# A second Strassen level in the aggregates of the second layer, panels 1 to 4

## The chip, the cores and the metric

One Trainium2 core runs the whole program. The metric is the device time of one execution in microseconds. TensorE (PE, with its weight loads shown apart as PEld) multiplies, VectorE (DVE) adds and evicts, ScalarE (ACT) does the exponentials and some copies, GpSimd (POOL) scales the aggregates and issues the stores, SyncE (SP) issues the loads.

## The reference

A graph network of two attention layers on 2708 nodes with 1024 features. Everything is float32, and the adjacency is a dense 2708 x 2708 integer matrix.

```python
def reference(x, adj, Wf, bf, Wg, bg, W0, bW, W1, a1, a2):
    h = maximum(layernorm(x), 0)
    f, g = h @ Wf + bf, h @ Wg + bg
    e = relu(f @ g.T)
    x = x + softmax(where(adj > 0, e, -9e15), axis=1) @ (h @ W0 + bW)
    h = maximum(layernorm(x), 0)
    hW = h @ W1
    e = leaky_relu(hW @ a1 + (hW @ a2).T, 0.2)
    x = x + relu(softmax(where(adj > 0, e, -9e15), axis=1) @ hW)
    return x
```

The second layer's scores are a sum of a column and a row, so its large products are two: the weights with `h` (the aggregate), and that with `W1` (the projection).

## The kernel before, in words

**Panels.** The destination nodes are cut into five panels, 0 to 4, with 576, 576, 532, 512 and 512 columns. The source nodes are 20 full tiles of 128 rows, which go in ten pairs (`NQ` = 10), and two left-over tiles, `MONO` and `TINY` (20 rows). For each panel of the second layer the kernel makes the exponentials of all source tiles (`weights1`, one item for each tile: two activations on ACT and three wide operations on DVE, into the tiles named P), then `aggregate`, then `project`. The items of the next panel's `weights1` are put into a list, `later`, and taken from it in pieces by `behind(us)`, which is called between the matmuls of the aggregate and of the projection of the panel at hand. `exps_until(n)` takes items until n are done.

**The aggregate** forms G = h^T P, with 1024 features by the panel's columns, in two halves of features (`gT` 0 and 1) of four chunks of 128. It is one level of Strassen's scheme in Winograd's form. In each pair the two source tiles a and b, the two feature halves and the two halves `lo` and `hi` of the columns make 2 x 2 blocks, and seven products M1 to M7 of half the width take the place of eight. The left sides of the seven are made once by `pair_h` and lie in DRAM (`hg_d`, one tensor for each two pairs); they are loaded as `hc`, 512 KB for two pairs, through a pool of 12 stream buffers (`strm`), in program order on SP. The right sides are sums of P, made on DVE in place: `T1` (wa hi minus wa lo), then `second` and `fourth`. Each product is 10 pairs times 4 chunks = 40 matmuls of 128 x 128 by half a panel (288, 266 or 256 columns), and accumulates in four PSUM banks. The order is M1, M5, M2, M6, M3, M7, M4. The results go out by `evict`, and the left-over tiles are added inside M2, M3, M4 and M7.

**The order of work.** PE, SP and DVE each run their queue in order. The order of DVE's queue is made beforehand by a scheduler that estimates when inputs are there; SP's is the program's. There are eight PSUM banks, 54 slots of a panel's width (`slots`), and 12 stream buffers.

**After the aggregate**, `scale` multiplies three quarters of `gT` with the inverse sums on POOL and the last quarter on DVE, and `project` multiplies with `W1`, again by one level of Strassen.

**Names that the change touches.** `pair_h` (left sides of the second layer), `left_h` and `left_over` (left-over tiles), `later`, `put`, `one`, `behind` (the list), `aggregate` (kept for the first layer and for panel 0 of the second), and the loop over panels at the end.

Of the kernel before, what the change touches and what calls it, by code (L numbers as in the profile page):

```python
# [18 lines left out]
P = 128  # L19
# [38 lines left out]
def kernel(  # L58
# [97 lines left out]
    assert sorted(group_of) == list(range(NQ))  # L156
    hg_d = [[dram.tile([P, 7, len(g), W], FP, name=f"hg{l}_d{i}") for i, g in enumerate(groups)] for l in range(2)]
    hsl_d = dram.tile([P, 2, NH, P], FP, name="hsl_d")
    hgl_d = [dram.tile([P, 2, W + P], FP, name=f"hgl{l}_d") for l in range(2)]
    md_d = dram.tile([P, 7, NH, W], FP, name="md_d")  # L160
# [21 lines left out]

    later, credit = [], [0.0]
    ahead = [5]

    def put(us, go, fetch=None, takes_psum=False, ready=None):
        later.append([us, fetch, go, takes_psum, ready])

    def one():
        for it in later[:ahead[0]]:  # L190
            if it[1]:
                it[1]()
                it[1] = None
        us, _, go = later.pop(0)[:3]
        go()
        return us

    def behind(us, psum_free=False):
        credit[0] = min(credit[0] + us, 2 * us)
        while later and credit[0] > 0 and (psum_free or not later[0][3]) and (not later[0][4] or later[0][4]()):  # L200
            credit[0] -= one()

    def flush():
# [97 lines left out]
    def left_h(l, hm, ht):  # L301

        for e in range(2):
            store(hgl_d[l][:, e, :W], hm[e])
            for d in range(NH):
                g = slice(B32 * d, B32 * (d + 1))
                store(hgl_d[l][g, e, W:], ht[e][g, d * P:(d + 1) * P])

    def pair_h(l, q, ha, hb):

        n = P
        on = nc.vector
        if q >= NQ - F // 2:
            s1, s2, s3, s4 = (slot(f"g{i}")[:, :W] for i in range(4))
            i, j = group_of[q]
            for m, h in ((M1, ha[0]), (M2, hb[0]), (M4, hb[1])):
                store(hg_d[l][i][:n, m, j], h)
            on.tensor_tensor(s1, ha[1], hb[1], OP.add)
            on.tensor_tensor(s2, s1, ha[0], OP.subtract)
            for m, h in ((M5, s1), (M6, s2)):  # L320
                store(hg_d[l][i][:n, m, j], h)

            def rest():
                on.tensor_tensor(s4, hb[0], s2, OP.subtract)
                on.tensor_tensor(s3, ha[0], ha[1], OP.subtract)
                for m, h in ((M3, s4), (M7, s3)):
                    store(hg_d[l][i][:n, m, j], h)
            return rest
        g1, g2 = stream("g1", (P, 2, W)), stream("g2", (P, 2, W))
        s1, s2, s3, s4 = g1[:n, 0], g1[:n, 1], g2[:n, 0], g2[:n, 1]  # L330
        on.tensor_tensor(s1, ha[1], hb[1], OP.add)
        on.tensor_tensor(s2, s1, ha[0], OP.subtract)
        on.tensor_tensor(s3, ha[0], ha[1], OP.subtract)
        on.tensor_tensor(s4, hb[0], s2, OP.subtract)
        i, j = group_of[q]
        for m, h in ((M1, ha[0]), (M2, hb[0]), (M4, hb[1])):
            store(hg_d[l][i][:n, m, j], h)
        store(hg_d[l][i][:n, M5:M6 + 1, j], g1[:n])
        store(hg_d[l][i][:n, M7:M3 + 1, j], g2[:n])

    def rows_h(q, ha, hb):

        i, j = group_of[q]
        for m, h in ((M1, ha[0]), (M5, ha[1]), (M2, hb[0]), (M4, hb[1])):
            store(hg_d[0][i][:, m, j], h)

    summed = [0]

    def sums_h():

        def fetch(q, two):
            i, j = group_of[q]
            for m in (M1, M2):
                two.append(stream("hr", (P, 2, W)))
                load(two[-1], hg_d[0][i][:, m:m + 2, j])

        def first(q, two):
            (a0, a1), (b0, b1) = ((t[:, 0], t[:, 1]) for t in two)
            add(b1, a1, b1)
            sub(a1, a0, a1)  # L360

        def second(q, two):
            (a0, a1), (b0, b1) = ((t[:, 0], t[:, 1]) for t in two)
            sub(a0, b1, a0)
            sub(b0, b0, a0)
            i, j = group_of[q]
            store(hg_d[0][i][:, M6:M7 + 1, j], two[0])
            store(hg_d[0][i][:, M3, j], b0)
            store(hg_d[0][i][:, M5, j], b1)
            summed[0] += 1  # L370
        for q in range(NQ):
            two = []
            put(1.4, lambda q=q, two=two: first(q, two), lambda q=q, two=two: fetch(q, two))
            put(1.4, lambda q=q, two=two: second(q, two))

    u = consts.tile([P, NC], FP, name="u")
# [464 lines left out]
    def aggregate(l, p, S, sm, then={}, rate=3.0):  # L841
# [28 lines left out]
        def left(m, q, d):  # L870
            i, j = group_of[q]
            if (m, i) not in hc:
                hc[m, i] = stream("hc", (P, 2, W))
                load(hc[m, i], hg_d[l][i][:, m])
            return hc[m, i][:, j, d * P:(d + 1) * P]

        def left_over(ps, e, s, start=False):


            two = stream("hl", (P, W + P))  # L880
            load(two, hgl_d[l][:, e])
            for d in range(NH):
                nc.tensor.matmul(ps[d], two[:, d * P:(d + 1) * P], S[MONO][:, s], start=start, stop=False,
                                 skip_group_check=True)
            for d in range(NH):
                g = slice(B32 * d, B32 * d + NY)
                nc.tensor.matmul(ps[d], two[g, W:], S[TINY][g, s], start=False, stop=start, skip_group_check=True)

# [42 lines left out]
        def scale():  # L931
            for e, s, k in ((0, slice(0, w), w), (1, hi, h)):
# [5 lines left out]
                                    M4: lambda ps: left_over(ps, 1, lo), (M7, NQ // 2): into_m15})  # L938
        nc.vector.tensor_tensor(of(1, lo), of(1, lo), by(lo, h), OP.mult)
        return [t.rearrange("p (c i) -> p c i", c=NH) for t in G]  # L940

# [338 lines left out]

    done_rows, first_mask, raise_later = {}, {}, []

    def rows_done(t, xt):
# [14 lines left out]
        if panel_of[t] == NP - 1:  # L1298
# [9 lines left out]
            else:  # L1308
# [4 lines left out]
                rest = []  # L1313
                make = lambda: rest.append(pair_h(1, q, *(done_rows[s] for s in pairs[q])))
                if q == NQ - 1:
# [4 lines left out]
                for p in range(1, NP):  # L1320
                    put_max(p, q)
            return

# [12 lines left out]
        elif whole:  # L1336
            put(2.7, lambda: pair_h(1, q, *(done_rows[s] for s in pairs[q])))
            put(0.0, met)

    def halves_of_tiny(name):  # L1340
# [201 lines left out]

    take_weights(0)
    for p in range(NP):
        S, sm = got["P"]
        then = {}
        if p + 1 < NP:
            then = {M3: lambda p=p: take_shifts(p + 1), M7: lambda p=p: take_weights(p + 1)}
        g = aggregate(1, p, S, sm, then, rate=4.0)
        project(1, p, g, finish1(p), by_pair=(p == NP - 1), rate=1.7)  # L1550

# [28 lines left out]
```

## Time and profile before

| | |
|---|---|
| time, median of 3 | 3132.92 us (3130.36 to 3140.1) |
| profiled span | 3135.8 us, 36310 instructions |
| PE busy | 3053.1 us, 97% |
| PE weight loads busy | 2266.1 us, 72% |
| DVE busy | 1835.6 us, 59% |
| ACT, POOL busy | 450.3 us and 427.3 us, 14% each |
| DMA | 666.04 MB, 212 GB/s on average |

An fp32 matmul stands in the profile as two records, each with a weight load of its own. [...] neighbours overlap; the rate of a run of records is read from the start of one group to the start of the next. The second layer runs from about 2157 us to the end: five aggregates of 132 to 152 us and five projections of 48 to 62 us. Busy time of an engine in a stretch counts overlapping instructions once.

### The profile page before, as it was taken

To read this page: it belongs to the slowest core of one execution; us is meant where nothing else is said; L and a number is where in the kernel's file an instruction comes from. 1 tells how busy PE (TensorE), PEld (TensorE's weight loads), DVE (VectorE), ACT (ScalarE), POOL (GpSimd) and SP (SyncE) were. 2 spreads that over 40 slices of the span, in tenths; PEclk is the share of its full clock that TensorE was granted. 3 is DMA by queue.
4 is the path that set the end of the run, shared out by engine and by line. 5 is a ranking of instruction groups with operands and counts; after the bars stand their busy time and mean duration, and the time that the engine had idled before them with its cause. 6 is when DMAs were issued, how large, how long until landed. Compare 5 with 4: busy or idle time off the path is not lost.

```text
span 3135.8 us, 36310 instructions
## 1 busy us (share of the span) xinstructions
PE 3053.1 (97%) x12694; PEld 2266.1 (72%) x12694; DVE 1835.6 (59%) x3767; ACT 450.3 (14%) x785; POOL 427.3 (14%) x654
## 2 busy tenths in 40 slices
PE   8998999899999999999999999998999999999998
PEld 4576777657877588886888885875757758678684
DVE  5766693776741686426973377758573571745612
ACT  3420020010200101101020002103131130311200
POOL 1421101310002110023000101021010020120202
PEclk9999999999999999999999999998999999999999
DMA  6989967988546796468955678597655565565655
GB/s 220 294 252 248 292 247 253 301 275 230 175 136 156 222 247 223 149 153 253 284 180 160 171 214 245 191 293 250 200 179 175 158 200 158 171 197 172 219 169 181
DMA packets 386278, 666.04 MB, mean 212 GB/s; under 512 B 171744, under 2 KB 212224, under 8 KB 386096
## 3 DMA queue, kind: packets, MB, share of 16 engines
q1 hardware_dynamic: 341936, 536.96, 56.9%
q0 software_dynamic: 44160, 126.76, 12.6%
q8 instruction: 101, 1.65, 0.2%
q14 instruction: 81, 0.66, 0.1%
HBM read 548.26 MB, written 115.30 MB: 212 GB/s over the span
## 4 chain that ended last, share of the span: by engine, by line
PE 81%; issue 6%; DVE 6%; DMA 5%; SPq 1%; POOL 1%; ACT 0%; POOLq 0%; DVEq 0%; ACTq 0%
PE gz L617 11%; PE gx L617 11%; PE gy L617 10%; PE sz L1140 6%; PE pz L1029 5%; PE gv L617 5%; PE sx L1140 4%; PE sy L1140 4%; PE px L1029 4%; PE py L1029 4%; PE M_ps L530 3%; PE qz L617 2%; PE qx L617 2%; PE qy L617 2%; DVE junk L45 1%
## 5 line engine op out<-in xcount | busy, mean ns | idle before, releaser
L1140 PE MATMUL sz<-B,As 128*128 128x288 f32 (+2 forms) x1200 | 295.9, 396 | 12.1 <-DVE st L45 7.9
L1140 PEld LDWEIGHTS sz<-B,As 128*128 128x128 f32 x1200 | 229.4, 192 | 63.1 <-DVE st L45 11.8
L933 POOL TENSOR_TENSOR gT<-gT,rr 128x2304 f32<-128x2304 f32 (+5 forms) x20 | 73.0, 3648 | 1081.4 <-DVE rr L45 979.3
L1140 PE MATMUL sx<-B,As 128*128 128x288 f32 (+2 forms) x800 | 201.5, 395 | 11.2 <-DMA As<-hs_d 9.1
L1140 PE MATMUL sy<-B,As 128*128 128x288 f32 (+2 forms) x800 | 199.3, 392 | 0.0
L617 PE MATMUL gz<-Sa,hc 128*128 128x288 f32 (+2 forms) x800 | 190.3, 399 | 5.9 <-DMA hc<-hg_d 5.9
L617 PE MATMUL gx<-P,hc 128*128 128x288 f32 (+2 forms) x800 | 187.0, 394 | 0.1
L617 PE MATMUL gz<-P,hc 128*128 128x288 f32 (+2 forms) x800 | 185.5, 392 | 0.0
L1140 PEld LDWEIGHTS sx<-B,As 128*128 128x128 f32 x800 | 152.5, 191 | 45.2 <-DMA As<-hs_d 10.1
L617 PE MATMUL gy<-T,hc 128*128 128x288 f32 (+2 forms) x800 | 184.2, 391 | 0.0
L617 PEld LDWEIGHTS gz<-Sa,hc 128*128 128x128 f32 x800 | 154.6, 194 | 40.0 <-DMA hc<-hg_d 6.4
L617 PEld LDWEIGHTS gx<-P,hc 128*128 128x128 f32 x800 | 152.4, 191 | 34.2 <-issue 3.7
L1140 PEld LDWEIGHTS sy<-B,As 128*128 128x128 f32 x800 | 152.3, 191 | 30.8
L617 PEld LDWEIGHTS gz<-P,hc 128*128 128x128 f32 x800 | 151.3, 190 | 31.6 <-issue 1.8
L617 PEld LDWEIGHTS gy<-T,hc 128*128 128x128 f32 x800 | 152.0, 190 | 30.5
L1029 PE MATMUL pz<-w,ps 128*128 128x512 f32 x320 | 142.1, 594 | 0.8 <-DVE pt L45 0.8
L1029 PE MATMUL py<-w,ps 128*128 128x512 f32 x320 | 141.9, 593 | 0.0
L1029 PE MATMUL px<-w,gT 128*128 128x512 f32 x320 | 141.0, 593 | 0.0
L143 POOL DMA_DIRECT2D out_dram<-x_res x180 | 89.2, 502 | 269.7 <-DVE x_res L45 264.5
L1029 PEld LDWEIGHTS pz<-w,ps 128*128 128x128 f32 x320 | 60.2, 190 | 77.1 <-issue 71.0
L1029 PEld LDWEIGHTS py<-w,ps 128*128 128x128 f32 x320 | 60.6, 190 | 75.5 <-issue 73.1
L530 PE MATMUL M_ps<-wgT,wfT 128*128 128x512 f32 x256 | 112.9, 597 | 1.6 <-ACT hsT L45 1.6
(319 smaller groups left out, 4894.9 us busy)
## 6 DMA issues: line engine op xcount, KB each, us to landing
hc<-hg_d SPq DMA_DIRECT2D x350, 512.0 KB, 3.7
As<-hs_d SPq DMA_DIRECT2D x150, 512.0 KB, 5.2
w<-wt_d SPq DMA_DIRECT2D x96, 512.0 KB, 4.9
w<-in_L_gnn_W_dram SPq DMA_DIRECT2D x72, 512.0 KB, 4.8
md<-md_d SPq DMA_DIRECT2D x56, 512.0 KB, 5.7
adj_i<-in_adj_dram SPq DMA_DIRECT2D x200, 128.0 KB, 5.2
hs_d<-hsT POOLq DMA_DIRECT2D x40, 512.0 KB, 7.2
As<-hs_d SPq DMA_DIRECT2D x50, 256.0 KB, 4.8
```

The source lines that it names most:

```text
L45: i = f(*a, **k)
L143: nc.gpsimd.dma_start(a, b)
L530: nc.tensor.matmul(ps, wfT[a][c // NH][:, c % NH, :], wgT[b][c], start=(c == 0), stop=(c == NC - 1))
L617: nc.tensor.matmul(ps[d], left(m, k, d), right(m, k), start=(start and k == 0), stop=(k == K - 1), skip_group_check=True)
L933: nc.gpsimd.tensor_tensor(of(e, s), of(e, s), by(s, k), OP.mult)
L1029: nc.tensor.matmul(ps, left[i][m][:, k, :], w_[k], start=(start and k == 0), stop=(k == NH - 1), skip_group_check=True)
L1140: nc.tensor.matmul(ps[:n, :h], lefts[q][:, i % 2, c, :n], B[m][c // 2][:, c % 2, :h], start=(start and c == 0), stop=(c == NH - 1), skip_g ...
```

## The change

For panels 1 to 4 of the second layer each of the seven products is split once more by the same scheme. Two neighbouring pairs (2k and 2k+1, so five k) are the inner dimension, each feature half is cut into two quarters of 256, and each half panel into two of 144, 133 or 128 columns. A product of 40 matmuls becomes seven of 5 x 2 = 10 matmuls of half the columns, which is 49 small products for each panel.

- `pair_h` writes its left sides as blocks into one tensor, `hr_d`, in pieces of 1 KB. `put_quarters` makes the four further left sums of each m and k: it loads 512 KB through POOL's queue, does four subtractions or additions of 128 x 256 on DVE, and stores 512 KB into `hs2_d`. These 35 items go into a second list, `lazy`, which is served when `later` is empty.
- `quarters_of` makes the right sides. `make(m)` does 5 x 4 subtractions of 128 x 144 (133, 128) for each of the seven m. The first set and the `T1` are made during the projection of the panel before.
- `aggregate_quartered` runs the 49 products. Each loads 512 KB (`hc2`) for four of the five k; the fifth comes from two further loads of 512 KB for each m (`hl2`, in pieces of 1 KB). A bank holds both chunks of one quarter. The results of M1 and M5 are built in their place in `gT`; those of the others in two tiles V, and then added to it.
- The calls of `behind` are one for each small product, with 1.2 us; the next panel's shifts and weights are taken at M7 and M3 in place of M3 and M7 (the order of the two has changed too).
- Panel 0 keeps the old aggregate, and reads the new layout.

```diff
+    hr_d = dram.tile([P, 7, 2, 2, NK, WH], FP, name="hr_d")
+    hs2_d = dram.tile([P, 7, 4, NK, WH], FP, name="hs2_d")
...
+        while not later and lazy and credit[0] > 0:
+            credit[0] -= one(lazy)
...
+    def put_quarters(m, k):
+        two = []
+        def fetch():
+            two.append(stream("hq", (P, 4, WH)))
+            nc.gpsimd.dma_start(two[0], hr_d[:, m, :, :, k].rearrange("p h f c -> p (h f) c"))
+        def go():
+            a11, a12, a21, a22 = (two[0][:, i] for i in range(4))
+            add(a22, a21, a22)
+            sub(a21, a11, a21)
+            sub(a11, a22, a11)
+            sub(a12, a12, a11)
+            store(hs2_d[:, m, :, k], two[0])
...
+        put(1.7, go, fetch, to=lazy)
...
+        def make(m):
+            for k in range(NK):
...
+                sub(t[M5], r12, r11)
+                sub(t[M6], r22, t[M5])
+                sub(t[M7], r22, r12)
+                sub(t[M4], r21, t[M6])
...
+        def product(m, n, ps, start):
+            quarters_until(m)
+            if (m, 0) not in lasts:
...
+                    lasts[m, i] = stream("hl2", (P, 4, WH))
+                    load(lasts[m, i], of)
+            t = stream("hc2", (P, NK - 1, WH))
...
+            for k in range(NK):
+                for d in range(2):
+                    lhs = t[:, k] if k < NK - 1 else last
+                    nc.tensor.matmul(ps[:, d], lhs[:, d * P:(d + 1) * P], inner_right(m, n, k),
+                                     start=(start and k == 0 and d == 0), stop=(k == NK - 1), skip_group_check=True)
+            behind(fine)
...
+        for m in BY_QUARTERS:
...
+            X = bank2("gx")
+            product(m, M1, X, True)
+            nc.scalar.copy(c21, X)
+            if left_out:
+                left_out()
+            Z = bank2("gz")
+            product(m, M6, Z, True)
+            add(c12, Z, c21)
+            Y = bank2("gy")
+            product(m, M5, Y, True)
+            add(c22, Y, c21)
...
+            if m in before_next:
+                before_next[m]()
+            product(m, M2, X, False)
...
+            product(m, M7, Z, False)
+            add(c22, Z, c22)
+            product(m, M3, Y, False)
...
+            add(c12, Y, c12)
...
+            into_place(m, V, 0)
+            def left_out(m=m, V=V, Z=Z, c21=c21):
+                product(m, M4, Z, False)
+                add(c21, Z, c21)
+                into_place(m, V, 1)
...
+            if m == M5:
+                of_right["second"]()
...
-        g = aggregate(1, p, S, sm, then, rate=4.0)
-        project(1, p, g, finish1(p), by_pair=(p == NP - 1), rate=1.7)
+        g = aggregate_quartered(p, S, sm, next_right, then) if p else aggregate(1, p, S, sm, then, rate=4.0)
+        hooks = {}
+        if p + 1 < NP:
+            next_right = quarters_of(p + 1, got["P"][0])
+            hooks = {M7: next_right["first"], M4: next_right["fifth"]}
+        project(1, p, g, finish1(p), hooks, by_pair=(p == NP - 1), rate=1.7)
```

## The prediction

> **What bounds the kernel now.** I read the page first (busy time and chain), then the busy time by stage, then the timelines of PE and DVE in single stages.
>
> ```profile
> PE 3053.1 (97%) x12694; PEld 2266.1 (72%) x12694; DVE 1835.6 (59%) x3767; ACT 450.3 (14%) x785; POOL 427.3 (14%) x654
> PE 81%; issue 6%; DVE 6%; DMA 5%; SPq 1%; POOL 1%; ACT 0%; POOLq 0%; DVEq 0%; ACTq 0%
> ```
>
> The chain that ended last is PE for 81%. By stage of the second layer, from panel 1 on (aggregate, projection, aggregate and so on; columns: length, then busy time of PE, PEld, DVE, ACT, POOL, then clock, DMA share, GB/s):
>
> ```profile
> 2357.10:2507.30 150.20, 150.20 (x645) 115.72 (x644) 63.64 (x123) 20.98 (x38) 11.60 (x10) 1.00 0.53 162
> 2507.30:2569.00 61.70, 61.70 (x145) 27.32 (x144) 40.81 (x63) 20.23 (x33) 14.12 (x29) 1.00 0.55 170
> 2569.00:2707.40 138.40, 138.40 (x641) 115.36 (x640) 59.02 (x118) 19.01 (x34) 11.47 (x12) 1.00 0.56 175
> 2707.40:2760.30 52.90, 52.90 (x241) 24.20 (x240) 38.60 (x63) 18.50 (x33) 19.99 (x40) 1.00 0.65 205
> 2760.30:2893.60 133.30, 133.30 (x641) 115.37 (x640) 57.34 (x117) 18.86 (x34) 10.81 (x10) 1.00 0.59 181
> 2893.60:2941.70 48.10, 48.10 (x114) 21.29 (x114) 38.19 (x60) 17.32 (x29) 11.85 (x24) 1.00 0.69 209
> 2941.70:3073.70 132.00, 132.00 (x630) 114.16 (x629) 34.59 (x79) 6.73 (x14) 10.79 (x10) 1.00 0.59 183
> ```
>
> PE has no gap in any of these stages, so what PE does not have to do is gained, unless something new makes it wait. DVE is busy 43% of an aggregate, but 80% of the short projections.
>
> The rate of PE, from panel 3, and short transposes from panel 2:
>
> ```profile
> 2777.58 17.43 PE L617 MATMUL gy<-T,hc 128*128 128x256 f32 x80
> 2794.84 13.98 PE L617 MATMUL gx<-P,hc 128*128 128x256 f32 x64
> ...
> 2685.95 0.60 PE L238 MATMUL sp_ps<-ident,z 128*128 128x128 f32 x4
> 2686.39 0.60 PE L238 MATMUL sp_ps<-ident,none 128*128 128x128 f32 x4
> ```
>
> From start to start 80 records of 256 columns take 17.26 us, 215.8 ns each. The same view gives 242.5 ns at 288 columns (19.40 us for 80) and 224.1 ns at 266 (17.93 us). The slope is (242.5 - 215.8)/32 = 0.834 ns a column, the rest 2.3 ns. The four transposes are 128 columns with a new weight tile each, and take 0.44/4 = 110 ns.
>
> DVE back to back, in panel 2 and in projection 0:
>
> ```profile
> 2573.22 3.20 DVE L45 TENSOR_TENSOR T<-P 128x266 f32<-128x266 f32 x9
> 2314.06 0.69 DVE L45 TENSOR_TENSOR ps<-ps,gT 128x512 f32<-128x512 f32 x1
> 2314.67 0.69 DVE L45 TENSOR_TENSOR ps<-gT 128x512 f32<-128x512 f32 x1
> 2315.27 0.68 DVE L45 TENSOR_TENSOR ps<-gT,ps 128x512 f32<-128x512 f32 x1
> ```
>
> One of 266 columns takes (3.20 - 0.43)/8 = 0.346 us from start to start, one of 512 takes 0.60. So an independent fp32 operation costs about 0.067 us and 1.05 ns a column: 0.20 us at 128 columns, 0.21 at 133, 0.22 at 144, 0.34 at 256, 0.37 at 288. One that needs its neighbour's result starts about 0.1 us later.
>
> [...] the weight loads of an fp32 pair stand 0.11 us apart where two follow each other ("26.73 0.30 ... x2" with 0.19 for one), though each lasts 190 ns. [...] The trace has 401 and 416 GB/s in stretches of 5 us at a share of 1.02.
>
> **PE, the gain.** An aggregate has 7 x 80 = 560 records now and 49 x 20 = 980 after, of half the columns. By the line above they take 122.4 ns at 144, 113.2 at 133, 109.1 at 128; [...] the transposes show 110 for such a pair. So panel 1 goes from 135.8 to 120.0 us, panel 2 from 125.5 to 110.9, panels 3 and 4 from 120.8 to 106.9: 15.8 + 14.6 + 13.9 + 13.9 = 58.2 us less. The left-over MONO matmuls have the same columns (twice as many at half width). The TINY ones, 0.71 us for eight now, become four short groups; I put 0.2 us more for each of four places, 3 us in all. Net 55.
>
> **DVE, what it adds.** A panel gets 140 subtractions of a quarter, 140 x 0.21 to 0.25 = 29 to 35 us. Evictions go from 28 of half a panel to 42 of the same size, and 16 twice as wide into place, which is 14 x 0.35 + 16 x 0.62 = 15 us. Aggregate 3 then has 57 + 32 + 15 - 3 (T1, moved) = 101 us of DVE work in about 107, and projection 3 has 38 + 4 + 3 = 45 in 48. It fits on average with little to spare, so the order decides.
>
> **The start of each quartered aggregate, the wait I expect.** The queue order of the changed program shows what lies ahead of the first eviction. In panels 2 to 4 DVE, after the last eviction of the projection (0.3 us into the aggregate), has: seven operations of exponential items, ten T1 subtractions, one x_res, three subtractions of `second` (10 us by the rows above), then 15 of the 20 quarter sums of M5 and two wide operations (5 us), and only then c12, the eviction of the M6 product. So c12 is done at about 15.4 us. PE needs it for the M7 product, which accumulates in the same bank, after M1, M6, M5 and M2: 4 x 2.18 = 8.7 us. PE waits 6.7 us. Behind it the M3 product waits 0.4 us for c22, the M4 product 0.2, the next M7 and M3 0.9 together, as DVE works off `second` (20 x 0.34) and the second set of sums; after 45 us DVE has caught up. That is 8.2 us for each of panels 2 to 4. In panel 1 only 13 operations more than the quarter sums stand ahead, c12 comes at 12 us and perhaps 2 later, against 4 x 2.45 = 9.8; with the follow-ups 5 us. Sum 30 us. What is queued behind c12 on DVE is exponentials and sums; ACT's copies of the next X wait with them, and mask loads on SP that need a freed slot, with `hc2` loads behind them.
>
> **Loads.** An aggregate's left sides go from 35 to 63 loads of 512 KB, +14.7 MB. Panel 3 moves 181 GB/s x 133 us = 24.1 MB now, 38.8 MB after, in about 115 us: 337 GB/s, against 401 to 416 measured at full share. Eight or so products of lookahead lie in the 12 buffers. I expect short waits, 1 us a panel: 4 us.
>
> **First layer and panel 0.** 35 items add 140 x 0.34 = 48 us of DVE and 36.7 MB of DMA, spread over 1500 us in which DVE is 60% busy; PE hides them, but where a list was empty an item's load and its first use are issued together, and DVE waits for a load of some 5 to 7 us in its queue. I take 3 us (0 to 10). The 1 KB pieces of `hr_d`, the wider `hgl`, the copies on ACT (19 of 133 us busy) and the POOL scaling (7 us, now issued some 14 us before the projection) lie beside PE work: nothing.
>
> **Sum.** 3132.9 - 55 + 30 + 4 + 3 = 3115 us.
>
> **Rivals.** (a) DVE is quicker than I count or its order harmless, and PE keeps nearly all: 3132.9 - 55 + 4 + 3 = 3085, down to 3078. For it: DVE's busy sum is under PE's time everywhere. Against: the order of the queue. Chance 0.22. (b) Small waits in many places, each product being only 2.2 us long where it was 17 to 20: with twice my DVE waits on panels 1 and 3 and 5 us more for loads, +18, so 3133, no change. Chance 0.14. (c) Transfers or weight loads become the bound. At 300 GB/s, the best of the 78 us slices, 38.8 MB take 129 us, and an aggregate of panel 3 or 4 ends 14 us later than I have it, panels 1 and 2 somewhat less: +45, so 3160. And if the weight loads (190 ns long) [...] set 125 ns a record, panels 2 to 4 would gain 3, -2 and -2 us and panel 1 would gain 13, 45 us lost: 3160. For both: a DMA share of 0.59 that would go to about 0.9, and no run of full-width fp32 pairs under 215 ns in this trace. Against: 401 GB/s and 110 ns are seen. Chance 0.22. The forecast itself has 0.42.
>
> **How the numbers follow.** The forecast is the sum with its DVE waits, 3115. The range reaches down to the full gain (3078, rounded to 3082) and up to the load-bound case with a part of it avoided, 3155. Faster by over 0.3% means under 3123.5: forecast and (a), 0.63 with the forecast's upper tail taken off and some of (b) added. Within 0.3%: 0.14. Slower: 0.23.
>
> **What would show each step.** PE records of 128 columns at 109 to 112 ns from start to start within a product (0.19 us would break the gain). In panels 2 to 4, a gap of PE of 5 to 8 us ahead of the second gz group of each aggregate, put down to DVE gT. An aggregate 3 of 107 + 9 us. A DMA share near 0.85 with few PE waits for hc. No new idle time in the projections and little before 2157 us. The forecast is wrong if PE waits for loads over 10 us a panel, or if DVE's gap is absent.

## The result, and the profile after

The changed kernel takes 3185.9 us (median of 4, 3176.1 to 3189.4) against 3131.6: a ratio of 1.0166, 95% interval 1.0142 to 1.0190. It is slower by 1.7%, where 3115 us and a gain were forecast.

Part 1 of the page of the changed kernel (busy time, share of the span, instructions), and the summary of its chain:

```profile
PE 3030.0 (95%) x14630; PEld 2319.2 (73%) x14630; DVE 2072.4 (65%) x4587; ACT 462.3 (15%) x817; POOL 488.9 (15%) x724
PE 69%; DVE 13%; DMA 9%; issue 6%; SPq 2%; ACT 1%; POOL 1%; POOLq 0%; DVEq 0%; ACTq 0%
```

PE is busy 23 us less and the profiled execution takes 52 us more, so PE waits: its share of the chain fell from 81 to 69%, and DVE and DMA took it. The busy time by stage of the second layer, the changed kernel (length, busy PE, PEld, DVE, ACT, POOL, clock, DMA share, GB/s). The first line is panel 0's aggregate, which is not split; the others answer to the lines shown of before:

```profile
2201.40:2368.02 166.62, 160.00 (x663) 121.61 (x664) 125.28 (x250) 41.74 (x71) 20.38 (x19) 0.95 0.70 225
2416.08:2565.30 149.22, 139.06 (x1128) 136.82 (x1127) 105.06 (x278) 19.54 (x39) 11.95 (x10) 0.95 0.79 251
2565.30:2627.10 61.80, 61.80 (x146) 27.36 (x145) 42.12 (x76) 17.99 (x29) 14.06 (x29) 1.00 0.63 197
2627.10:2762.51 135.41, 127.41 (x1126) 125.48 (x1125) 103.24 (x274) 24.18 (x45) 12.17 (x12) 0.97 0.84 276
2762.51:2815.41 52.90, 52.90 (x243) 24.20 (x242) 39.40 (x76) 16.46 (x29) 19.88 (x40) 1.00 0.73 231
2815.41:2948.61 133.20, 125.18 (x1125) 123.47 (x1124) 100.75 (x274) 23.77 (x45) 11.49 (x11) 0.97 0.87 286
2948.61:2996.68 48.07, 48.07 (x114) 21.29 (x113) 38.25 (x69) 16.04 (x26) 11.79 (x24) 1.00 0.74 234
2996.68:3127.18 130.50, 123.00 (x1114) 121.45 (x1112) 84.06 (x247) 15.76 (x32) 11.07 (x10) 0.97 0.88 288
```

Two things are to be seen. The second layer starts at 2201.40, where before it started at 2147.94: the loss of 53.5 us is complete before the first split product runs, and panel 0's aggregate adds 5.5 (161.1 before). And the four split aggregates gain almost nothing: 150.2, 138.4, 133.3, 132.0 became 149.2, 135.4, 133.2, 130.5, together 5.6 us. Their PE time fell by 8 to 11 us each, but PE no longer fills the stage, and the clock is 0.95 to 0.97. The four projections shown or named here are as long as before (48.1, 61.8, 52.9 and 48.1 us); what follows the last aggregate went from 62.1 to 60.4 us.

**What PE waits for in the first layer.** From the view of PE's waits up to 2201 us (us in total, times, longest), first after, then before. `sx`, `px` and the like are PSUM banks of the scores and the projection:

```profile
PE sx L1368 <- DMA As<-hs_d: 34.7, 8, 9.2
PE px L1257 <- DMA w<-in_L_gnn_W_dram: 16.5, 1, 16.5
```
```profile
PE sx L1140 <- DMA As<-hs_d: 9.1, 2, 8.1
```

The left sides `As` of the scores and the weights `w` come late. Up to the start of the second layer PE is idle 40 us longer than before, and its 8760 records, as many as before, keep it busy 13 us longer (2095.8 us against 2082.7); together that is the 53.5. The instants are those at which the new items (`put_quarters`) run: their 35 loads stand in the trace at 698 to 719, 1159 to 1188, 1564 to 1595, 2093 to 2113 and 2233 to 2288 us, seven at a time, and 23 us of the `As` waits end at 715, 735, 1170 to 1206 and 1592, the `w` wait at 2148; the other 11.7 come before the first item, as the 9.1 of before do. Busy time in the first two of these stretches (columns as above), after, then before, and in the first of them in the run `spread` told below:

```profile
690.00:740.00 50.00, 39.70 (x140) 28.99 (x139) 41.07 (x93) 0.00 (x0) 14.38 (x20) 0.87 0.98 297
1150.00:1205.00 55.00, 45.91 (x202) 37.66 (x200) 47.49 (x106) 0.00 (x0) 13.59 (x18) 0.96 1.01 299
```
```profile
690.00:740.00 50.00, 48.41 (x192) 37.37 (x193) 39.40 (x87) 0.00 (x0) 4.16 (x7) 0.97 0.96 258
1150.00:1205.00 55.00, 55.00 (x247) 46.63 (x246) 37.65 (x83) 0.00 (x0) 2.86 (x4) 1.00 0.97 284
```
```profile
690.00:740.00 50.00, 49.27 (x204) 38.31 (x203) 36.28 (x74) 0.00 (x0) 2.71 (x6) 1.00 0.93 250
```

The DMA engines were full here before the change: a share of 0.96 and 0.97, though at 258 and 284 GB/s only. A burst of seven items adds 7.3 MB to that, PE loses 9 us of busy time in each stretch, and the granted clock falls, to 0.87 in the first.

**What PE waits for in a split aggregate.** The seven small products of a product bear the names M1 to M7 too, and run in the order M1, M6, M5, M2, M7, M3, with M4 put behind the first one of the next group; "the M5 group" below is the seven of the large M5, the second group of an aggregate. c21, c12 and c22 are quarters of a group's result. PE's timeline at the start of panel 1's aggregate, then ScalarE's and VectorE's over the same time (rows left out):

```profile
2420.99 2.12 PE L1059 MATMUL gy<-quarter,hc 128*128 128x144 f32 x16
2431.92 4.21 PE L1059 MATMUL gx<-P,hc 128*128 128x144 f32 x16 [8.32 <-ACT gT L45]
2436.83 2.12 PE L1059 MATMUL gz<-quarter,hc 128*128 128x144 f32 x16
```
```profile
2424.81 0.76 ACT L45 ACTIVATE P<-vb,f2s 128x576 f32<-128x576 f32 x1
2430.90 0.68 ACT L45 ACTIVATE P<-P 128x576 f32<-128x576 f32 x1 [5.33 <-DVE P L45]
2431.49 0.38 ACT L45 COPY gT<-gx 128x288 f32<-128x288 f32 x1
```
```profile
2425.55 3.03 DVE L45 TENSOR_TENSOR T<-P 128x288 f32<-128x288 f32 x8
2429.16 0.81 DVE L45 SCALAR_TENSOR_TENSOR P<-ub,f,P 128x576 f32<-128x576 f32 x1
2430.11 0.75 DVE L45 TENSOR_TENSOR P<-P,maskl 128x576 f32<-128x576 f32 x1
```

The fourth small product (M2) adds into the bank of the first, so it needs that bank copied out to c21. The product ended at 2418.7. ScalarE copies it only at 2431.5: in its queue an exponential stands ahead, which waits for the masking that VectorE ends at 2430.9, and VectorE works through the sums of M1, T1 and other exponentials without a pause. PE waits 8.3 us here, and 6.1, 6.1 and 7.1 us in panels 2 to 4. And when it starts, 16 records take 4.21 us and not 2.12: half speed, for 4.9 us, at a granted clock of 0.50 (2432 to 2436 us).

### The profile page after: what moved, and what is told of

The parts are those of the page before. It is cut to its first block, busy times and chain, and to the rows that moved or that the text cites. A ratio compares the mean times of both kernels' runs of the same rounds, so it can differ in the third digit from the quotient of the medians.

```text
span 3187.6 us, 41503 instructions
## 1 busy us (share of the span) xinstructions
PE 3030.0 (95%) x14630; PEld 2319.2 (73%) x14630; DVE 2072.4 (65%) x4587; ACT 462.3 (15%) x817; POOL 488.9 (15%) x724
## 4 chain that ended last, share of the span: by engine, by line
PE 69%; DVE 13%; DMA 9%; issue 6%; SPq 2%; ACT 1%; POOL 1%; POOLq 0%; DVEq 0%; ACTq 0%
PE sz L1368 5%; PE gy L654 5%; PE gz L1059 5%; PE gx L654 5%; PE gz L654 5%; PE pz L1257 4%; PE px L1257 4%; PE sx L1368 4%; PE gx L1059 4%; PE gy L1059 3%; PE py L1257 3%; PE sy L1368 3%; PE M_ps L567 3%; PE gv L654 2%; PE qz L654 2%
## 5 line engine op out<-in xcount | busy, mean ns | idle before, releaser
L1368 PE MATMUL sx<-B,As 128*128 128x288 f32 (+2 forms) x800 | 209.7, 407 | 36.5 <-DMA As<-hs_d 34.7
L1059 PE MATMUL gz<-quarter,hc 128*128 128x128 f32 (+2 forms) x1344 | 168.8, 279 | 0.4 <-DVE gT L45 0.4
L1059 PEld LDWEIGHTS gz<-quarter,hc 128*128 128x128 f32 x1344 | 160.9, 191 | 1.2 <-DVE gT L45 0.6
L1257 PE MATMUL py<-w,ps 128*128 128x512 f32 x320 | 142.0, 593 | 0.0
L970 POOL TENSOR_TENSOR gT<-gT,rr 128x2304 f32<-128x2304 f32 (+5 forms) x12 | 44.4, 3699 | 560.1 <-DVE rr L45 522.0
L1257 PEld LDWEIGHTS px<-w,gT 128*128 128x128 f32 x320 | 61.2, 194 | 89.6 <-issue 87.8
L1059 PE MATMUL gx<-P,hc 128*128 128x128 f32 (+2 forms) x640 | 88.2, 295 | 27.6 <-ACT gT L45 27.6
L654 PE MATMUL gy<-T,hc 128*128 128x288 f32 (+2 forms) x480 | 111.6, 394 | 0.0
L1059 PEld LDWEIGHTS gx<-P,hc 128*128 128x128 f32 x640 | 83.6, 204 | 31.6 <-ACT gT L45 28.4
```

The lines of the kernel that those rows point to most:

```text
L654: nc.tensor.matmul(ps[d], left(m, k, d), right(m, k), start=(start and k == 0), stop=(k == K - 1), skip_group_check=True)
L970: nc.gpsimd.tensor_tensor(of(e, s), of(e, s), by(s, k), OP.mult)
L1059: nc.tensor.matmul(ps[:, d], lhs[:, d * P:(d + 1) * P], inner_right(m, n, k), start=(start and k == 0 and d == 0), stop=(k == NK - 1), ski ...
L1257: nc.tensor.matmul(ps, left[i][m][:, k, :], w_[k], start=(start and k == 0), stop=(k == NH - 1), skip_group_check=True)
L1368: nc.tensor.matmul(ps[:n, :h], lefts[q][:, i % 2, c, :n], B[m][c // 2][:, c % 2, :h], start=(start and c == 0), stop=(c == NH - 1), skip_g ...
```

## The experiments

Each kernel below was timed beside the kernel before, whose median was 3128.3 to 3133.2 us in these sessions, so medians of different sessions are best compared by their ratios. Stage lengths come from PE's timeline of one profiled execution of each, as the distance between the first records of stages; "first" is the start of the second layer, a0 to a4 are its aggregates. Panels 2 to 4 repeat to 0.4 us between kernels that do the same there, panel 1 to 2.3. The first layer's end moves by some 8 us between such kernels, and the whole time of one kernel by 12 (3121.7 to 3134.3 in the 12 executions of `spread`). The first four projections kept 48.1, 61.8, 52.9 and 48.1 us in all of them.

| run | median us | ratio, 95% interval | first | a0 | a1 | a2 | a3 | a4 |
|---|---|---|---|---|---|---|---|---|
| before | 3131.6 | 1 | 2147.9 | 161.1 | 150.2 | 138.4 | 133.3 | 132.0 |
| changed | 3185.9 | 1.0142-1.0190 | 2201.4 | 166.6 | 149.2 | 135.4 | 133.2 | 130.5 |
| no_items | 3118.8 | 0.9964-0.9985 | 2135.3 | 161.8 | 147.4 | 135.4 | 133.2 | 130.5 |
| copies | 3159.2 | 1.0089-1.0119 | 2176.1 | 162.0 | 147.6 | 135.4 | 133.1 | 130.5 |
| own_bufs | 3219.1 | 1.0282-1.0313 | 2233.0 | 162.0 | 149.7 | 135.4 | 133.2 | 130.5 |
| spread | 3126.6 | 0.9981-1.0005 | 2146.2 | 161.3 | 149.7 | 135.4 | 133.2 | 130.5 |
| own12 | 3223.4 | 1.0264-1.0297 | 2239.4 | 162.0 | 148.9 | 135.8 | 133.5 | 130.4 |
| no_items_10 | 3136.9 | 1.0005-1.0023 | 2162.7 | 160.9 | 148.7 | 135.6 | 133.4 | 130.5 |
| burst_late | 3163.8 | 1.0094-1.0127 | 2130.2 | 199.5 | 149.7 | 135.4 | 133.2 | 130.5 |
| spread_start | 3147.3 | 1.0034-1.0051 | 2147.4 | 161.6 | 143.8 | 145.1 | 141.9 | 134.1 |
| spread_warm | 3157.8 | 1.0054-1.0084 | 2148.5 | 161.9 | 151.0 | 143.0 | 140.6 | 138.6 |
| no_sums | 3113.7 | 0.9938-0.9967 | 2144.4 | 161.6 | 146.5 | 133.2 | 131.5 | 126.8 |
| pool_t1 | 3155.8 | 1.0069-1.0103 | 2147.3 | 161.1 | 154.4 | 141.7 | 140.4 | 137.8 |
| pool_both | 3168.8 | 1.0114-1.0145 | 2147.0 | 160.9 | 157.6 | 145.5 | 147.3 | 140.7 |
| early | 3143.7 | 1.0031-1.0061 | 2147.3 | 161.3 | 154.6 | 139.2 | 137.2 | 130.5 |
| whole1 | 3116.9 | 0.9945-0.9974 | 2152.5 | 161.8 | 140.8 | 134.1 | 132.8 | 129.1 |
| whole2 | 3107.1 | 0.9918-0.9948 | 2145.1 | 161.7 | 141.9 | 130.5 | 127.8 | 124.1 |
| best2 | 3101.3 | 0.9896-0.9929 | 2141.1 | 161.2 | 142.0 | 130.5 | 127.8 | 124.1 |

### The first layer: items, bytes, buffers or layout

**no_items**

```diff
-        put(1.7, go, fetch, to=lazy)
+        return
...
-            load(t, hr_d[:, m, i // 2, i % 2, :NK - 1] if raw else hs2_d[:, m, i, :NK - 1])
+            load(t, hr_d[:, m, i // 2, i % 2, :NK - 1])
```

> Left out: the quarter sums of the left sides (the 35 items that load a group of hr_d, subtract and store hs2_d); the products that would read hs2_d read hr_d in its place, so loads, matmuls and evictions of the second layer are as many as in the changed kernel. The layout of hr_d in pieces of 1 KB stays. Theory A (the tiles of the items hold places of the 12 load buffers, and the one load queue waits in order for them) and theory B (their 36.7 MB come when the DMA engines are full): the first layer ends at 2148 us as before and not at 2201, whole time about 3133, and 5 us less if the first aggregate of the second layer is relieved too. Theory C (the layout, 1 KB pieces instead of 2 KB, slows the stores): the first layer still ends near 2195, whole time about 3180.

3118.8 us, 67 less than the changed kernel (60 by the ratios). The items cost the whole of the loss; the layout of `hr_d` costs nothing (theory C falls). That this first layer ends 12.6 us earlier than before was not expected and stays unexplained; part of it may be the scatter.

**copies**

```diff
         def fetch():
-            two.append(stream("hq", (P, 4, WH)))
-            nc.gpsimd.dma_start(two[0], hr_d[:, m, :, :, k].rearrange("p h f c -> p (h f) c"))
+            nc.gpsimd.dma_start(hs2_d[:, m, :, k], hr_d[:, m, :, :, k].rearrange("p h f c -> p (h f) c"))
         def go():
-            a11, a12, a21, a22 = (two[0][:, i] for i in range(4))
...
-            store(hs2_d[:, m, :, k], two[0])
+            nc.gpsimd.dma_start(hs2_d[:, m, :, k], hr_d[:, m, :, :, k].rearrange("p h f c -> p (h f) c"))
```

> Changed in content: each item copies its group from hr_d to hs2_d twice, inside DRAM, with no tile, no DVE work and no sums; the bytes queued are as in the changed kernel (512 KB twice an item). Theory A (buffers): with no tile in the ring the first layer ends near 2150, whole time about 3135. Theory B (transfers): the engines have the same to move at the same moments, so the first layer ends near 2195, whole time about 3180.

3159.2, between the two: transfers alone, with no tile and no sum, cost 40 us over no_items. That price is near that of the items' own transfers and not the same: a copy reads and writes DRAM both times (35 times 512 KB, 18 MB, more each way), and the second doesn't wait for sums. The rest, 19 us by the ratios and 27 by the medians, belongs to the tiles, the sums and the waits between them.

**own_bufs**, **own12** and **no_items_10**

The edit is that of own_bufs. own12 keeps 12 buffers in `strm` and takes the room from `slots` (51 in place of 54); no_items_10 is no_items with 10 buffers in `strm`.

```diff
-    strm = ctx.enter_context(tc.tile_pool(name="strm", bufs=12))
+    strm = ctx.enter_context(tc.tile_pool(name="strm", bufs=10))
+    hqs = ctx.enter_context(tc.tile_pool(name="hqs", bufs=2))
...
-            two.append(stream("hq", (P, 4, WH)))
+            two.append(hqs.tile([P, 4, WH], FP, tag="hq", name="hq"))
```

> The tiles of the items get 2 buffers of their own, and the ring of loads has 10 in place of 12. Theory A: the load queue no longer waits for the stores of hq; most of the 53 us come back, whole time 3140 to 3150 (the smaller ring may cost some). Theory B: the same transfers at the same moments, 3180 to 3190.

> The tiles of the items get 2 buffers of their own, and the ring of loads keeps its 12; the room comes from the slots, 51 in place of 54. The run of copies showed that the bytes alone cost 40 us over the run without items, and the changed kernel 67; this asks after the other 27. Theory A2 (places of the ring held by hq until the stores have landed): 3155 to 3165. Theory H (VectorE's 48 us of sums, in program order in the scores, and waiting for their loads): 3180 to 3190.

> The run without items (quarter sums of the left sides left out, hr_d read in the place of hs2_d) with a ring of 10 load buffers in place of 12. If places of the ring are what is scarce in the first layer, this alone costs some 35 us and more (3118 to 3150 or above), and explains why 2 buffers of their own for the items made the time longer, 3219. If a place more or less costs nothing, 3118 to 3124, and that run needs another cause.

Both kernels with buffers of their own are slower than the changed one, by 33 and 38 us (41 and 36 by the ratios): theory A failed as it was put. A ring of 10 explains some 12 us by the ratios (0.9974 to 1.0014; 18 by the medians), but own12 has the ring of 12. Its waits from 600 to 2260 us show what happened instead:

```profile
DVE hq L45 <- DMA hq<-hr_d: 87.6, 19, 10.3
```
```profile
PE sx L1369 <- DVE sm L45: 46.6, 8, 15.8
```

In the changed kernel these are 9.4 and 1.8 us. The load queue's waits for the items' stores fell from 42.3 to 1.9 us, and none of PE's waits in the scores is for `As` any more. But a burst of seven now goes through two places: in the first one, loads 3 to 7 are issued at 722 to 749 us, each 4 to 8 us after a store was issued (714 to 742 us). VectorE, whose order is the written one in the scores, stands before these loads with the right sides `sm` and the evictions of the scores behind it, and PE waits for those. So these runs exchange one wait for another, and how the last 19 to 27 us divide between ring and VectorE stays open; in own12 the three slots fewer may cost some as well.

**spread**

```diff
-        while not later and lazy and credit[0] > 0:
-            credit[0] -= one(lazy)
...
             if by_k:
                 behind(rate)
+                in_gaps(2 if rate == 4.0 else 1)
```

> All computed as in the changed kernel; the items no longer run in a burst of seven when the list is empty, but one after each of the seven products of a first-layer aggregate, and two after each product of the second layer's first aggregate, where DVE and DMA have room (DMA share 0.55 to 0.65 there before, 0.9 to 1.0 at the start of the scores). Theories A and B alike: the waits for As and w go, the first layer ends at 2150 to 2158, the first aggregate of the second layer takes 161 to 168 us, whole time 3135 to 3145. Theory C: about 3180. A burst that moves its waits to hc loads of the aggregates would show as waits of gx, gy, gz for hc.

3126.6, with all that the changed kernel computes: some 8 us better than both theories had it. The first layer ends at 2146.2, panel 0's aggregate is 161.3 as before. The waits of the load queue and of VectorE for the items are longer than ever:

```profile
SPq L139 <- DMA hs_d<-hq: 159.2, 31, 12.3
```
```profile
DVE hq L45 <- DMA hq<-hr_d: 86.7, 16, 9.7
```

The load queue waits 159 us for stores of the items, where it waited 68 in the changed kernel, and VectorE stands 87 us before their loads, as long as in own12. The kernel is within 8 us of the one without items all the same: no wait of PE for `As` is left after 600 us, and one of 4.7 us for `w`. What an item holds is not the price; what stands behind it at that moment is.

**burst_late**

```diff
-                in_gaps(2 if rate == 4.0 else 1)
+                in_gaps(0 if m != M5 else 14 if rate == 4.0 else 7)
```

> In the run with spread items, the items come in bursts of seven again, but behind the second product (M5) of each first-layer aggregate, where the DMA share was 0.5 to 0.65 before, and 14 in one go at the same place of the second layer's first aggregate. Theory N (it is the place: at the start of the scores the DMA engines were already full, and PE has little loaded ahead): the first layer ends at 2145 to 2155 as with spread items, whole time 3125 to 3140. Rival O (it is the burst itself: seven items take places of the ring and delay what is behind, wherever they stand): the first layer ends at 2175 or later, with waits of gx, gy, gz for hc, whole time 3155 or more.

Theory N in the first layer: bursts of seven, at 852, 1250 and 1628 us, where the DMA share was 0.44 to 0.48 before, and the first layer ends at 2130 (in an execution 11 us under the median, so perhaps 2141). The 14 at once in panel 0's aggregate cost 38 us (199.5), with waits for `hc` there that `spread` doesn't have:

```profile
PE gx L657 <- DMA hc<-hr_d: 24.8, 3, 17.4
```

So a burst of seven cost nothing that shows where the engines had that room. The 14 differ in size and in place, and which of the two makes their price wasn't tried.

### The second layer: the wait at the start of an aggregate

All of these stand on `spread`.

**spread_start**

```diff
-            behind(fine)
...
-        before_next = {M1: lambda: make(M5), M5: with_second,
+        before_next = {M1: lambda: of_right["fifth"](), M5: with_second,
...
+            nc.hold = ("vector", "scalar") if m == M1 else ()
             product(m, M1, X, True)
             nc.scalar.copy(c21, X)
+            behind(fine)
...
```

> The run with spread items, and in each quartered aggregate another order of the first seven products: items of exponentials are called after the evictions, not before; the ten subtractions of `fifth` come after c22 of the M5 product and the sums of M5 after the second c22; VectorE and ScalarE keep that written order through the first group. Theory D (the copy of the first small product to c21 stands on ScalarE behind an exponential that waits for VectorE, and PE waits 8.3, 6.1, 6.1 and 7.1 us for it, then runs some 5 us at half clock): all four gaps fall under 1 us, each aggregate of panels 1 to 4 is 8 to 11 us shorter, 149.7 to 139, 135.4 to 127, 133.2 to 125, 130.5 to 122, whole time 3126 - 36 = 3090. Rival E (VectorE as a whole has too much to do; the wait comes back at the next eviction): the gaps move to gz or gy and the aggregates keep 147, 133, 131, 129; whole time 3118 to 3126.

Rival E. Panel 1 gained 5.9 us, its gap fell from 8.3 to 1.0. In panel 2 the first gap went too, and 8.2 us came at c21 of the next group, M5, whose copy stood again behind an exponential that waited for VectorE; the last M3 product of panels 1 to 3 waited some 5 us in place of 1 to 2. Panels 2 to 4 lost 9.7, 8.7 and 3.6.

**spread_warm**

```diff
+            if m == M1:
+                dull = bank("dull")
+                for _ in range(26):
+                    nc.tensor.matmul(dull[:, :P], ident, ident, start=True, stop=True, skip_group_check=True)
             product(m, M2, X, False)
```

> The run with spread items, and 26 matmuls of the identity by itself (52 records, 5.7 us by 110 ns) that nothing reads, put into a bank of their own ahead of the product that waits for c21 in each quartered aggregate. They fill the gap and remove none of it. Theory F (the half clock after a gap is a cost of its own, some 2.4 us a gap): the product after starts as late as before but at full clock, each aggregate of panels 1 to 4 is 2 to 2.5 us shorter (149.7 to 147.4, 135.4 to 133, 133.2 to 130.9, 130.5 to 128.2), 9 us in all, though PE has more to do. Rival G (the slow records belong to the busy memory, not to the clock): the products after the gap stay at twice their time and the aggregates are as long as before or longer.

The half speed is the clock's (0.50 granted over the 3.8 us after this gap in the changed kernel): in panel 2 the wait for c21 shrank to 0.31 us and the 16 records behind it took 2.08 us where 6.1 us of waiting had made them 3.9 (rival G falls). In panel 1, where 2.50 us of waiting were left, the 16 records still took 3.72 us. But nothing was won. PE came to the next eviction earlier and waited 1.76 us there, and 5.82 us in the M5 group; the aggregate was 7.6 us longer. VectorE's order moved with the added matmuls as well, so this run doesn't price the clock.

**no_sums**

```diff
-                four = slot("quarter", (P, 4, WX // 4))
...
+                t = {}
...
```

> Left out: the 140 subtractions of a panel that make the quarter sums of the right sides (the products read the quarters themselves); all else as in the run with spread items, with the same matmuls, loads and evictions. Theory K (VectorE works without a pause over the first 30 us of a quartered aggregate, 40 of the sums among it, so PE waits for it wherever one looks; moving the wait or the clock does not help, removing VectorE work does): the four gaps of 6 to 8 us and the half clock after them go, the aggregates take 149.7 to 137-139, 135.4 to 124-127, 133.2 to 121-124, 130.5 to 119-121, whole time 3126 - 45 = 3080. Rival L (the gap is the order on ScalarE alone, exponentials and T1 still stand ahead of c21): gaps of 4 us remain and the aggregates lose 5 to 6 us each, 3103.

Nearer to rival L: gaps of 5.1, 4.0, 3.9 and 3.8 us in place of 8.3, 6.1, 6.1 and 7.1, about as it has them, and 1.7 to 3.7 us an aggregate, less than it has. So the sums made some 11 us of the 27.6; the other 17 stay when they are gone, and exponentials and T1 are what is left ahead of c21.

**pool_t1** and **pool_both**

```diff
-                sub(t1(q), wa_(q)[:, hi], wa_(q)[:, lo])
+                nc.gpsimd.tensor_tensor(t1(q), wa_(q)[:, hi], wa_(q)[:, lo], OP.subtract)
```

> The ten T1 subtractions of a panel (`fifth`) on GpSimd in place of VectorE, in the run with spread items; VectorE has 3.8 us less ahead of the first evictions. Theory K: each gap shrinks by 3 to 4 us, the aggregates by 4 to 5 us, whole time about 3110. If GpSimd's own queue (stores of the output rows that wait for VectorE stand ahead) brings T1 late, the wait moves to the sums of M5 and nothing is won: 3125 to 3135.

> As the run before, and the 20 quarter sums of M1 on GpSimd too: 8.8 us off VectorE around the start of each quartered aggregate. GpSimd scales 1024 columns in 2.34 us, so 20 sums of 128 to 144 columns should take some 8 to 10 us there. Theory K: gaps near 0 and aggregates of 140, 127, 125, 122, whole time about 3095. Against it: the M6 product, the second of an aggregate, needs these sums 2.2 us after the start, and if GpSimd has them late PE waits for it instead: 3125 to 3150.

pool_both moves the sums of M1 as well. Both lose, 29 and 42 us on `spread`. The timeline of pool_t1, GpSimd beside VectorE:

```profile
2364.65 1.56 POOL L1023 TENSOR_TENSOR T<-P 128x288 f32<-128x288 f32 x2
2364.72 2.11 DVE L45 TENSOR_TENSOR sm<-sm,P 128x576 f32<-128x576 f32 x1
...
2369.71 6.02 POOL L1023 TENSOR_TENSOR T<-P 128x288 f32<-128x288 f32 x8
2370.55 5.87 DVE L45 TENSOR_TENSOR P<-P 128x288 f32<-128x288 f32 x2 [2.01 <-POOL T L1023]
```

A sum of 576 columns that takes 0.75 us elsewhere took 2.11 beside GpSimd, and two of 288 took 5.87 us where two take 0.81. While GpSimd subtracts here, VectorE stands, and not for want of T: neither of those rows of VectorE reads it, and the one wait of VectorE for T between 2340 and 2400 us is the 2.01 us before the second. What holds VectorE in these 5.87 us was not shown.

**early**

```diff
-            then = dict(zip((M7, M3) if p else (M3, M7), (lambda p=p: take_shifts(p + 1), lambda p=p: take_weights(p + 1))))
+            then = dict(zip((M6, M7) if p else (M3, M7), (lambda p=p: take_shifts(p + 1), lambda p=p: take_weights(p + 1))))
```

> In the run with spread items, the exponentials of the next panel are queued one product earlier (shifts at M6 and weights at M7 in place of M7 and M3), into the middle of the aggregate, where VectorE is busy 40 to 65% of the time. Theory K: some six exponentials (2.3 us of VectorE each) leave the end of the projection, the gaps fall to 0 to 3 us, aggregates of 142, 128, 126, 123, whole time about 3098. Rival: their tiles find no free slot until the last products have read theirs (54 slots for two panels of 22), VectorE waits in order, and the gaps move to gz and gy in M3 and M4: 3120 to 3150.

The rival: the gaps at c21 stay (8.3, 5.5, 5.5, 6.5) and waits of 3.3 us come at the left-over of M4 in panels 1 to 3. 17 us slower than `spread`.

**whole1** and **whole2**

```diff
+            if m in WHOLE:
+                product_whole(m, before_next[m])
...
+                continue
             V = [quad(*direct[m])[:, 2 * r:2 * r + 2] for r in range(2)] if m in direct else ...
```

> In the run with spread items, the first of the seven products (M1) of each quartered aggregate stays one half-wide product, as in the kernel before (80 records, 17.3 to 19.4 us where the seven small ones take 15.6 to 17.2), and its quarter sums of both sides fall away (30 items for 35). PE has 1.7 to 2.3 us more a panel, VectorE 5 us of sums and six evictions less, and 17 us pass before PE needs anything that VectorE has yet to make. Theory K (VectorE's heap at the start of an aggregate): the gaps of 6 to 8 us and the half clock after go, and nothing takes their place; the aggregates take 149.7 to 142, 135.4 to 129, 133.2 to 127, 130.5 to 125, whole time about 3126 - 26 = 3100. Rival M (VectorE has too much over the whole of projection and aggregate, wherever it stands): the wait comes back in the M5 group, 3118 to 3130.

> As the run before, with M5 one half-wide product too: PE 3.4 to 4.6 us more a panel than with all seven split, VectorE 10 us of sums less and 35 us before it is needed. If one whole product is enough, this is the slower of the two by 8 us in all, 3108; if VectorE's heap reaches into the second group (rival M), it is the faster, about 3105 against 3120.

Leaving M1 whole freed panel 1 (140.8, no gap over 0.9 us at its start), but in panels 2 to 4 a wait of 3.7 to 4.0 us came back in the M5 group (rival M), and with M5 whole it is gone as well. PE's timeline of whole2 at the start of panel 3:

```profile
2742.01 17.43 PE L1074 MATMUL gx<-P,hc 128*128 128x256 f32 x80
2759.28 17.43 PE L1074 MATMUL gx<-T,hc 128*128 128x256 f32 x80
2776.55 1.95 PE L1063 MATMUL gx<-P,hc 128*128 128x128 f32 x16
2778.33 0.61 PE L1063 MATMUL gx<-P,hl 128*128 128x128 f32 x4
2778.78 1.95 PE L1063 MATMUL gz<-quarter,hc 128*128 128x128 f32 x16
```

No gap, and full speed. A whole product takes 17.27 us from start to start; a small one 2.23, and seven of them 15.6. So each product left whole gives up 1.65 us of the gain, and with two of them VectorE has 35 us to work off what it has before PE needs it. Less of the idea is worth more: 5.5 us an aggregate gained on before in panel 3, where splitting all seven gained 0.1.

**best2**

```diff
-                in_gaps(2 if rate == 4.0 else 1)
+                in_gaps(2 if rate == 4.0 else 5 if m == M5 else 0)
```

> The run with M1 and M5 whole, with its items (five of a group there) in one burst behind M5 of each first-layer aggregate, and two after each product of the second layer's first aggregate as in that run. If the burst is free in the first layer's aggregates and the short stretches of prefetch in the spread form cost some us, 3095 to 3107; if the two forms are the same in the first layer, 3107.

3101.3 us, 0.9912 of the kernel before (0.9896 to 0.9929). It beats both kernels: the one before by 28 us, the changed one by 80 to 85. That with the burst the whole is 6 us shorter than whole2 is within what the first layer moves by itself.

## Why the prediction was wrong

**The step that failed: "First layer and panel 0 ... spread over 1500 us in which DVE is 60% busy; PE hides them ... I take 3 us (0 to 10)".** It measured 53.5 + 5.5 = 59 us. The items were not spread. `lazy` is served when `later` is empty, and that is so some 30 to 70 us into a stage of scores (three groups) and at the end of the first layer's last aggregate (one); there all seven of a group go within 20 to 40 us. I judged room by VectorE's average over the layer; the view that decides was the DMA share of those 50 us in the kernel before, 0.96, and it could be read. spread, with the same items at another time, is 8 us above no_items, and burst_late shows no cost of its 21 items in the first layer. So it is shown that the place of the items makes the price; how the last 19 to 27 us divide between ring and VectorE is not.

**The start of each quartered aggregate** was right in its kind and its size and wrong in its place: 30 us forecast, 33.7 us of waits measured (27.6 for c21, 6.1 at other evictions, nearly all late in the aggregate). I had PE wait at the second gz product for VectorE's c12; it waits one product earlier, at gx for c21, since ScalarE's copy stands in order behind an exponential that waits for the same VectorE. I named ScalarE's copies as waiting "with them" and did not ask who needs the first.

**A term that was missing: the clock.** Each gap of 6 to 8 us is followed here by records at half speed, at a granted clock of 0.50 over 3.6 to 4.0 us in panels 1 to 3 and of 0.56 over 3.3 us in panel 4. Summed over the products after the gaps, each against its time in the same stage (2.45, 2.27 or 2.23 us), that is 4.2, 2.5, 2.5 and 2.1 us, 11 in all (an estimate from the starts of records). In the first layer, after the waits for `As` and `w`, the same records took 13 us longer than before; how much of that is the clock wasn't separated. The forecast had no term for it. From what length on a wait brings it was not shown: 1.84 us brought slow records too in the changed kernel (16 in 3.79 us, at a clock of 0.56) and not in whole2 (2.23 us), and in panel 1 of spread_warm 2.50 us did (3.72 us) and 3.26 us did not (2.23 us).

**PE, the gain.** 122.5 ns at 144 columns and 113.3 at 133, against 122.4 and 113.2: right. At 128 columns 111.6 (2.23 us for 20), not 109.1: 2.5 us a panel, 5 in all, less gain in panels 3 and 4. The transposes' 110 stood beside the line and the larger of the two wasn't taken. The left-overs take at most 0.5 us a panel more than they took.

**Loads.** No wait for `hc` or `hl2` in any quartered aggregate, at a DMA share of 0.79 to 0.88: 0 in place of 4 us.

So the four aggregates: the forecast's 21 us of gain, less 11 for the clock, 5 for the pitch and 4 for longer waits, plus 4 for the loads, leaves 5, and 5.6 were measured. With the 56 us that the items cost over their term these 15 make up the 71 us between 3115 and 3186. Of the rivals, (c) named transfers, but in the second layer's aggregates, which lost nothing to loads; that its 3160 lay nearest is luck.

## What to carry to other kernels

Work that "fits on average" has to be placed: look up the DMA share and the VectorE share in the 50 us in which a queue will really issue it, not over the layer. A gap of PE cost its length here and then the slow records behind it (8.3 us, then 16 records in 4.21 us in place of 2.12), and it was set by whichever queue the first needed eviction stood in. How long a queue waits is not its price: 159 us of the load queue and 87 of VectorE cost next to nothing in `spread`, and the same 87 us of VectorE made PE wait in own12. When a faster PE outruns the engine that feeds it, apply the change to the part that the other engine can keep up with: with the items placed alike, splitting five products of seven gained 22 us and splitting all seven 2, which is not clear of the noise.

## What the runs showed of the hardware

Beside GpSimd's subtractions VectorE's took far longer in pool_t1 (5.87 us for two of 288 columns that take 0.81 elsewhere), so an idle GpSimd was no spare VectorE for them here. The DMA engines were full at 258 GB/s in the scores (a share of 0.96) and carried 401 GB/s in other stretches (2205 to 2210 us of before, a share of 1.02), so here their share said if there was room, and the rate didn't. After a wait of 8.3 us PE's granted clock was 0.50 for at least 4 us. Pairs of a weight load and a 128-column record follow each other at 111.6 ns over 20 records, not the 110 of a set of four.
